# Plain products for the last pairs' spreads, second power and layer 1, a wider turn through DRAM, and a last pair finished tile by tile

## The chip, the cores and the metric

One core of a Trainium2 chip runs the whole kernel. The metric is the device time of one execution in microseconds (us), as the median of several runs. A profile is of one execution. Its span runs from the program's first to its last instruction on the core, and the execution's own time is a little longer.

## The reference

The input `x` is 64 graphs of 256 nodes and 128 features, `adj` one 256x256 matrix for all. Four graph layers follow each other, each wrapped as `x = layernorm(x + layer(x))`, all in fp32. The lines that matter here:

```python
# layer 0: a gated recurrence, five steps, with m = adj @ h
z = sigmoid(av @ w3_w.T + w3_b + u3); r = sigmoid(av @ w4_w.T + w4_b + u3)   # av = [m, m]
hv = tanh(av @ w5_w.T + w5_b + (r * h @ u5_w.T + u5_b)); h = (1 - z) * h + z * hv
# layer 1: A is a softmax over the edges' values, split in its diagonal and the rest
out = (A * I) @ (x @ W[0]) + (A * (1 - I)) @ (x @ W[1]) + bias
# layer 2: attention over adj, then a graph isomorphism layer with adj
# layer 3: a polynomial in adj of order 3, for two adjacencies that are the same one here
y = sum over k of (adj^k x) @ weight[k]
```

## The kernel before

Two graphs are a pair, and 32 pairs pass through the four layers. A pair's value is 512 columns on 128 partitions: four tiles of 128 nodes by 128 features (graph 0 first and second half, graph 1 first and second half), or their transposes.

**Order of the work.** The functions emit nothing at once. Each adds an operation with an estimated duration and the values that it reads and writes (`pe`, `act`, `dve`, `pool`, `S.add`). `Schedule.order` then lists them for all engines by a plan: of the operations that are ready it takes the one that could start first, and among these the one with the earliest due time. Due times are 15 us apart from pair to pair (10 for the last twelve) with an offset by layer (`HOLD`; layer 3 has 40 us). `SEEDS` shifts due times in windows of 15 us of planned time, a number for each window. Each engine then executes its list in order, so an instruction that waits holds back all behind it on that engine. Tiles are shared: 38 of 512 columns (A), 6 wider ones (B), 8 PSUM banks (PS), 8 DRAM buffers (E). Some operations have a choice of engines (`evacuate`: ACT or DVE; `dve_or_pool`, `sum_`: DVE or POOL).

**Spreads.** A product with a 256x256 matrix is a "spread". The plain form (`spread`, L591) has four matmuls of 256 columns. The block form (`spread7`, L609) takes seven 128-column products of sums of blocks instead of eight; the sums before are L615 to L617, those after L624, L628 and L630, and `evacuate` (L273 on ACT, L274 on DVE) copies partial results out of PSUM. `spread_on7` (products L1011, sums L1017 to L1019 and L1028 to L1032) does the same for the second power of `adj`, on top of what is already in a bank. `SEVEN` says how many of the last pairs take plain forms: `q1` layer 1's spread, `g` layer 2's, `q3` layer 3's, `a2` the second power, `pr` layer 3's weight products, which else go by `polynomial7` (products L968).

**Layer 1.** `layer1` spreads `x1`, scales `x1` by the diagonal (L808), turns that, puts `x1` and the bias into a PSUM bank (`seed`) and adds eight weight products (L764). `layer1b` multiplies the turned `x1` by both weights first (L779) and spreads after (L790). Before, `L1 = -1`, and no pair takes `layer1b`.

**Turns.** A transposition (`turn`) of most values goes through DRAM: DVE transposes 32x32 blocks (L572), one DMA stores the tile (L574), four DMAs load it back (L580), all issued by SP. The last few pairs of some sites use TensorE (L566). Site "y" is the last turn of layer 0, whose result L755 adds to `x0`; 30 pairs turn there by DMA.

**The last pair.** It goes through plain products for its two halves of the nodes (L906, L907; second power L914), and `finish` does each half: a square with its sum on ACT (L934), the variance on DVE (L937, L938), an addition (L940) and a power (L941) on POOL, the scaling on ACT (L942) and DVE (L943), and a store (L944).

Of the kernel before, what the change touches and what calls it, by code (L numbers as in the profile page):

```python
# [12 lines left out]
P = 128  # L13
# [7 lines left out]


FAST = (0, 1, 2, 3, 4)
SEVEN = {"q1": 4, "g": 4, "q3": 4, "pr": 2, "a2": 2}
FIRST, FINAL = 1, 0
L1 = -1

TURN, TT = 0.44, 0.61
LN_EPS = 1e-5
# [30 lines left out]

XLOAD, TLOAD = (0.6, 1.33, 2.5), (0.6, 1.05, 1.5)

SEEDS = [0, 113, 389, 2033, 10562, 18537, 0, 26210, 32078, 38683, 45160, 51706, 59435, 64921, 73141, 0, 83634, 0,
         0, 101285, 106383, 115324, 122347, 124837, 135500, 136596, 144091, 154692, 155685, 163406, 167552, 0,
         184910, 185838, 194559, 198013, 204219, 214550, 217961, 222675, 234550, 236036, 241268, 247877, 256254,
         259921, 269567, 275378, 0, 285335, 290367, 299853, 303332, 311190, 314874, 321452, 333089, 337426,
         340720, 349168, 0, 0, 0, 0, 0, 0, 0, 0, 0, 0, 0, 0, 426668, 0, 438032, 447771, 0, 460174, 0, 468597,
         475031, 0, 0, 497766, 503314, 0, 0, 520395, 524746, 0, 0, 545845, 549434, 555392, 562168, 571415, 574768,
         578884, 0, 0]


def mm(cols, n=1):
# [4 lines left out]
class Value:  # L77
# [3 lines left out]
    def __init__(self, cls=None, ap=None, name="v"):  # L81
        self.cls, self.ap, self.name = cls, ap, name
        self.writers, self.readers, self.left = [], [], 0


        self.seeded = self.full = False

    def at(self, *shape):

# [150 lines left out]
def kernel(ctx: ExitStack, tc: tile.TileContext, x, xT, adj, adjT, mats, cols, rows, out):  # L240
# [14 lines left out]
    def act(us, fn, r, w):  # L255
        S.add([("ACT", us, fn)], r, w)

    def dve(us, fn, r, w):
        S.add([("DVE", us, fn)], r, w)

    def dve2(us, fn, r, w):
        S.add([("DVE+", us, fn)], r, w)

    def pool(us, fn, r, w):
        S.add([("POOL-", us, fn)], r, w)
# [257 lines left out]
    def bank():  # L523

        t = Value("PS", name="ps")
        t.full = True
        return t
# [29 lines left out]
    def turn(i, name, site, n=512):  # L557


        o = Value("A", name=name) if n == 512 else i  # L560
        if not by_dma(site):
            ts = [Value("PS", name="ps") for _ in range(n // 512)]
            for k, t in enumerate(ts):
                def fn(k=k, t=t):
                    for c in range(4):
                        nc.tensor.transpose(tokens(t)[:, c, :], i.at(n // P, P)[:, 4 * k + c, :], ident.ap)  # L566
                pe(TURN, fn, [i, ident], [t])
            for k, t in enumerate(ts):
                evacuate(lambda k=k: o.at(n)[:, 512 * k:512 * k + 512], lambda t=t: t.at(512), [t], [o])
            return o  # L570
        st, d = Value("A" if n == 512 else "B", name="turn"), Value("E", name="turn")
        dve(n / 512 * 0.55 + 0.09, lambda: nc.vector.transpose(st.at(n), i.at(n)), [i], [st])  # L572
        blocks = lambda *ap: bass.AP(tensor=d.ap.tensor, offset=d.ap.offset, ap=ap)
        S.add([("SP", 0.52, lambda: nc.sync.dma_start(blocks([P, P], [P * P, n // P], [1, P]), st.at(n // P, P)))],  # L574
              [st], [d], (0.6, n / 512 * 0.86, 0.5))

        def move():
            for q in range(4):
                b = blocks([P, 32], [32 * P, n // 32], [1, 32])
                nc.sync.dma_start(o.at(n // 32, 32)[32 * q:32 * q + 32],  # L580
                                  bass.AP(tensor=b.tensor, offset=b.offset + 32 * q, ap=b.ap))
        S.add([("SP", 2.1 if n == 512 else 2.7, move)], [d], [o], (-0.8, n / 512 * 1.5, 0.9))
        return o

    def spread(i, right):
# [134 lines left out]
    def layer0(x0, hT):  # L720
        h = x0
        for s in range(STEPS):
            mT = spread7(h, aT, aT7) if s in FAST and FIRST <= S.pair < n_pairs - FINAL else to_sbuf(spread(h, aT), "mT")
            t = bank()

            def reset(t=t, hT=hT, mT=mT):
                nc.tensor.matmul(t.at(512), mat("u3"), hT.at(512), start=True, stop=False)  # L727
                nc.tensor.matmul(t.at(512), w4.ap, mT.at(512), start=False, stop=True)  # L728
            pe(mm(512, 2), reset, [Wg, w4, hT, mT], [t])
            r, z, new = (Value("A", name=n) for n in ("r", "z", "hT"))  # L730
            act(0.59, lambda t=t, r=r: nc.scalar.activation(r.at(512), t.at(512), AF.Tanh, bias=bzrh.ap[:, 1:2], scale=0.5),  # L731
                [t, bzrh], [r])
            dve2(TT, lambda r=r, hT=hT: nc.vector.scalar_tensor_tensor(r.at(512), r.at(512), 1.0, hT.at(512),
                                                                      op0=ALU.add, op1=ALU.mult), [r, hT], [r])
            pe(mm(512), lambda t=t, mT=mT: nc.tensor.matmul(t.at(512), w3.ap, mT.at(512), start=False, stop=True,  # L735
                                                            skip_group_check=True), [w3, mT, t], [t])
            act(0.59, lambda t=t, z=z: nc.scalar.activation(z.at(512), t.at(512), AF.Tanh, bias=bzrh.ap[:, 0:1], scale=0.5),  # L737
                [t, bzrh], [z])
            t = bank()

            def candidate(t=t, mT=mT, r=r):
                nc.tensor.matmul(t.at(512), w5.ap, mT.at(512), start=True, stop=False)  # L742
                nc.tensor.matmul(t.at(512), u5h.ap, r.at(512), start=False, stop=True)  # L743
            pe(mm(512, 2), candidate, [w5, u5h, mT, r], [t])

            act(0.59, lambda t=t: nc.scalar.activation(t.at(512), t.at(512), AF.Tanh, bias=bzrh.ap[:, 2:3]), [t, bzrh], [t])  # L746
            dve(TT, lambda t=t, hT=hT: nc.vector.tensor_sub(t.at(512), t.at(512), hT.at(512)), [t, hT], [t])
            dve(TT, lambda t=t, z=z: nc.vector.scalar_tensor_tensor(t.at(512), z.at(512), 1.0, t.at(512),
                                                                   op0=ALU.add, op1=ALU.mult), [t, z], [t])
            dve(TT, lambda t=t, hT=hT, new=new: nc.vector.scalar_tensor_tensor(  # L750
                new.at(512), t.at(512), 0.5, hT.at(512), op0=ALU.mult, op1=ALU.add), [t, hT], [new])
            hT = new
            h = turn(hT, "h", "h" if s < STEPS - 1 else "y")
        y = Value("A", name="y")
        dve2(TT, lambda: nc.vector.tensor_add(y.at(512), h.at(512), x0.at(512)), [h, x0], [y])  # L755
        layer_norm(y, x0)

    def products(lefts, rights, t=None):
# [132 lines left out]
    def layer3(x3, p):  # L891
        xT = turn(x3, "xT", "x3")
        qT = spread7(x3, aT, aT7) if S.pair < n_pairs - SEVEN["q3"] else to_sbuf(spread(x3, aT), "qT")
        if S.pair < n_pairs - SEVEN["pr"]:
            return polynomial7(xT, qT, p)

        rr, o = Value("A", name="rr"), Value("A", name="o")
        ts = []
        for i in range(2):
# [11 lines left out]
        for i, t in enumerate(ts):  # L911
# [2 lines left out]
                    nc.tensor.matmul(t.at(512)[:, :N], a2T.ap[:, j, i * P:(i + 1) * P], rr.at(2, N)[:, j],  # L914
                                     start=False, stop=(j == 1), skip_group_check=True)
            pe(mm(256, 2), fn, [a2T, rr, t], [t])
        if S.pair == n_pairs - 1:
            for i, t in enumerate(ts):
                finish(t, Value("A", name="last"), i, p)
            return  # L920
        s, rs = scale_stats([(t, range(i, 4, 2)) for i, t in enumerate(ts)])
        for i, t in enumerate(ts):
            scale_tokens(t, o, range(i, 4, 2), s, rs)
        store(o, p)

    def finish(t, o, i, p):

        s, st, junk = Value("S", name="ms"), Value("S", name="st"), Value("A", name="junk")
        v = lambda b: t.at(2, D)[:, b, :]
        mv = lambda b: s.at(32)[:, 2 * b:2 * b + 2]  # L930
        var, rs = (lambda: s.at(32)[:, 1:4:2]), (lambda: s.at(32)[:, 4:6])
        half = lambda b: o.at(2, D)[:, b, :]
        m0, m1, r0, r1 = Part(s), Part(s), Part(o), Part(o)
        act(0.26, lambda: nc.scalar.activation(junk.at(D), v(0), AF.Square, scale=D ** -0.5, accum_out=mv(0)[:, 1:2]), [t], [m0, junk])  # L934

        def by_dve():
            nc.vector.bn_stats(st.at(6), v(1))  # L937
            nc.vector.bn_aggr(mv(1), st.at(6))  # L938
        dve(0.27, by_dve, [t], [m1, st])
        pool(0.2, lambda: nc.gpsimd.tensor_scalar(rs(), var(), LN_EPS, None, op0=ALU.add), [m0, m1], [s])  # L940
        pool(0.7, lambda: nc.gpsimd.tensor_tensor(rs(), rs(), neg_half.ap[:, :2], op=ALU.pow), [s, neg_half], [s])  # L941
        act(0.26, lambda: nc.scalar.mul(half(0), v(0), rs()[:, 0:1]), [t, s], [r0])  # L942
        dve(0.2, lambda: nc.vector.tensor_scalar(half(1), v(1), rs()[:, 1:2], None, op0=ALU.mult), [t, s], [r1])  # L943
        S.add([("SP", 0.52, lambda: nc.sync.dma_start(out[2 * p:2 * p + 2, i * P:(i + 1) * P].rearrange("b p d -> p b d"), o.at(2, D)))],  # L944
              [r0, r1], [], (0.6, 0.5, 0.9))

    def polynomial7(xT, qT, p):

# [141 lines left out]
```

## Time and profile before

| | |
|---|---|
| median of 3 runs | 1477.62 us (1476.7 to 1477.91) |
| the profiled execution's own time | 1476.42 us |
| its span | 1474.2 us |
| PE busy | 1462.0 us, 99% |
| DVE busy | 1293.2 us, 88% |
| ACT busy | 1078.7 us, 73% |
| POOL busy | 1010.0 us, 69% |
| DMA: packets, volume, share of 16 engines | 946868, 216.70 MB, 71% |
| granted TensorE clock, mean | 0.999 |

PE is TensorE's matmuls, PEld its weight loads, DVE VectorE, ACT ScalarE, POOL GpSimd, SP the engine that issues the DMAs. "L609" is line 609 of the kernel before. A row of the timeline or of a group names the engine, the line, the operation, what it writes and reads ("ps<-aT,a"), shapes and a count; in brackets stands how long the engine was idle before it and what released it. A matmul in fp32 shows as two instructions. Ends of matmuls are modelled, and neighbours overlap in the record, so their starts tell more than their busy time.

### The profile page before, as it was taken

The numbers are of one execution on the slowest core, as the hardware profiler recorded it, in microseconds if no ns is written. First come the engines' busy times: TensorE is split into PE (matmuls) and PEld (weight loads), VectorE is DVE, ScalarE is ACT, GpSimd is POOL, SyncE is SP. The second block draws the span as 40 slices with busy tenths as digits, with TensorE's granted clock in tenths as the row PEclk, the third lists the DMA queues.
The fourth block names the chain that finished last, engine by engine and source line by source line (L and its number), as shares of the span: only waits on it lengthen the run. The fifth ranks groups of instructions, "written<-read, shape, count | busy, mean of one in ns | idle before, by whom it ended". The sixth has DMA issues, their size and how long they took to land.

```text
span 1474.2 us, 29700 instructions
## 1 busy us (share of the span) xinstructions
PE 1462.0 (99%) x8274; PEld 1068.6 (72%) x8274; DVE 1293.2 (88%) x3185; ACT 1078.7 (73%) x3315; POOL 1010.0 (69%) x1574
## 2 busy tenths in 40 slices
PE   9999999999999999999999999999999999999998
PEld 6565666667667777777668777667777677778997
DVE  7877878889999989999988988888999889899995
ACT  3444556667788788878766887666788777889896
POOL 4422445566677788877658787657778788779875
PEclk9999999999999999999999999999999999999999
DMA  7544565767788898778786677675897777766653
GB/s 227 115 103 87 119 130 117 155 133 157 152 166 168 180 187 161 164 152 165 160 157 140 143 171 159 124 152 124 170 177 158 156 146 149 160 138 135 127 106 93
DMA packets 946868, 216.70 MB, mean 147 GB/s; under 512 B 726032, under 2 KB 942224, under 8 KB 946704
## 3 DMA queue, kind: packets, MB, share of 16 engines
q1 hardware_dynamic: 946704, 214.81, 71.3%
q8 instruction: 66, 1.08, 0.3%
q14 instruction: 98, 0.80, 0.2%
HBM read 116.86 MB, written 97.85 MB: 146 GB/s over the span
## 4 chain that ended last, share of the span: by engine, by line
PE 93%; DVE 3%; POOL 2%; ACT 1%; DMA 1%; issue 1%; SPq 0%; POOLq 0%; ACTq 0%; DVEq 0%
PE ps L609 24%; PE ps L735 9%; PE ps L742 9%; PE ps L743 9%; PE ps L727 9%; PE ps L728 9%; PE ps L764 7%; PE ps L968 6%; PE ps L864 3%; PE ps L1011 3%; PE ps L591 2%; PE ps L824 2%; POOL s L696 1%; DVE b L839 0%; POOL s L651 0%
## 5 line engine op out<-in xcount | busy, mean ns | idle before, releaser
L609 PEld LDWEIGHTS ps<-aT,a 128*128 128x128 f32 x2208 | 297.3, 192 | 78.2 <-issue 69.1
L273 ACT COPY a<-ps 128x128 f32<-128x128 f32 (+2 forms) x618 | 259.5, 442 | 105.2 <-PE ps L609 49.2
L609 PE MATMUL ps<-aT,a 128*128 128x128 f32 x2208 | 324.3, 275 | 0.5 <-ACT x L708 0.5
L731 ACT ACTIVATE a<-ps,bzrh 128x512 f32<-128x512 f32 x160 | 110.5, 691 | 102.4 <-PE ps L728 92.8
L746 ACT ACTIVATE ps<-ps,bzrh 128x512 f32<-128x512 f32 x160 | 106.2, 664 | 98.0 <-PE ps L743 95.6
L628 POOL TENSOR_TENSOR a<-a 128x128 f32<-128x128 f32 x206 | 105.2, 516 | 90.8 <-DVE a L624 80.1
L742 PE MATMUL ps<-a,w 128*128 128x512 f32 x320 | 163.8, 594 | 0.0
L728 PE MATMUL ps<-a,w 128*128 128x512 f32 x320 | 163.4, 592 | 0.0
L743 PE MATMUL ps<-a,u5h 128*128 128x512 f32 x320 | 163.4, 592 | 0.0
L735 PE MATMUL ps<-a,w 128*128 128x512 f32 x320 | 162.8, 594 | 0.1
L630 DVE TENSOR_TENSOR a<-ps,a 128x256 f32<-128x256 f32 x239 | 99.1, 417 | 71.0 <-ACT a L273 42.1
L688 ACT ACTIVATE a<-ps 128x128 f32<-128x128 f32 x504 | 133.1, 289 | 29.7 <-PE ps L764 13.4
L572 DVE STREAM_TRANSPOSE a<-a 128x512 f32<-128x512 f32 x215 | 149.4, 699 | 3.7 <-POOL a L1028 0.5
L696 POOL TENSOR_TENSOR s<-s,neg_half 128x4 f32<-128x4 f32 x127 | 142.4, 1122 | 6.8
L764 PE MATMUL ps<-W,a 128*128 128x128 f32 x1024 | 142.1, 275 | 0.1
L624 POOL TENSOR_TENSOR a<-a 128x256 f32<-128x256 f32 x123 | 92.0, 750 | 72.9 <-ACT a L273 72.1
L764 PEld LDWEIGHTS ps<-W,a 128*128 128x128 f32 x1024 | 130.3, 192 | 14.5 <-issue 12.4
L737 ACT ACTIVATE a<-ps,bzrh 128x512 f32<-128x512 f32 x160 | 110.8, 692 | 37.4 <-PE ps L735 34.3
L727 PE MATMUL ps<-a,W 128*128 128x512 f32 x256 | 131.0, 593 | 0.9 <-ACT a L273 0.9
L615 POOL TENSOR_TENSOR a<-a 128x256 f32<-128x256 f32 x97 | 72.3, 746 | 64.8 <-DMA a<-e 44.2
L743 PEld LDWEIGHTS ps<-a,u5h 128*128 128x128 f32 x320 | 60.8, 190 | 76.5 <-issue 64.8
L728 PEld LDWEIGHTS ps<-a,w 128*128 128x128 f32 x320 | 60.8, 190 | 76.5 <-issue 65.3
(255 smaller groups left out, 3650.7 us busy)
## 6 DMA issues: line engine op xcount, KB each, us to landing
e<-a SPq DMA_DIRECT2D x277, 256.0 KB
a<-e SPq DMA_DIRECT2D x1108, 64.0 KB
e<-b SPq DMA_DIRECT2D x32, 512.0 KB
b<-e SPq DMA_DIRECT2D x128, 128.0 KB
x<-x_in SPq DMA_DIRECT2D x32, 256.0 KB
t<-xT_in SPq DMA_DIRECT2D x32, 256.0 KB
a<-d SPq DMA_DIRECT2D x32, 256.0 KB
y_out<-a SPq DMA_DIRECT2D x31, 256.0 KB
```

What stands on the lines that cost most here:

```text
L273: S.add([("ACT", us[0], lambda: nc.scalar.copy(o(), i())), ("DVE", us[1], lambda: nc.vector.tensor_copy(o(), i()))], r, w)
L572: dve(n / 512 * 0.55 + 0.09, lambda: nc.vector.transpose(st.at(n), i.at(n)), [i], [st])
L609: pe(mm(128), lambda: nc.tensor.matmul(blk(t, k), left(), rt(), start=start, stop=True, skip_group_check=True), [*r, right, terms, *[t] * ...
L688: nc.scalar.activation(tokens(junk)[:, c, :], v.at(len(tiles), D)[:, k, :], AF.Square, scale=D ** -0.5, accum_out=mv()[:, c, 1:2])
L696: pool(1.02, lambda: nc.gpsimd.tensor_tensor(rs(), rs(), neg_half.ap, op=ALU.pow), [s, neg_half], [s])
L727: nc.tensor.matmul(t.at(512), mat("u3"), hT.at(512), start=True, stop=False)
L728: nc.tensor.matmul(t.at(512), w4.ap, mT.at(512), start=False, stop=True)
L735: pe(mm(512), lambda t=t, mT=mT: nc.tensor.matmul(t.at(512), w3.ap, mT.at(512), start=False, stop=True, skip_group_check=True), [w3, mT, t ...
L737: act(0.59, lambda t=t, z=z: nc.scalar.activation(z.at(512), t.at(512), AF.Tanh, bias=bzrh.ap[:, 0:1], scale=0.5), [t, bzrh], [z])
L742: nc.tensor.matmul(t.at(512), w5.ap, mT.at(512), start=True, stop=False)
L743: nc.tensor.matmul(t.at(512), u5h.ap, r.at(512), start=False, stop=True)
L764: nc.tensor.matmul(tokens(t)[:, c, :], tokens(i)[:, c, :], w(), start=(first and k == c == 0), stop=(k == len(lefts) - 1), skip_group_chec ...
```

## The change

Four constants change, and three pieces of code. `a2` goes from 2 to 12: pairs 20 to 29 take the second power by plain products inside `polynomial7`. `q3` goes from 4 to 8: pairs 24 to 27 take layer 3's spread in the plain form. `L1` goes from -1 to 4: pairs 28 to 31 take `layer1b`. `SEEDS` has other numbers from its sixth place on.

`wide_turn` replaces the turn by DMA of site "y": the blocks are written by DVE in another order, so that the store has runs of 512 elements and the loads runs of 128 instead of 32. The value that comes back has its blocks permuted, and the addition after it (L755) reads it by a permuted pattern.

`by_tile` replaces the last pair's products: each of the four tiles gets a bank of its own, the right-hand factors of the second power are made and copied out first, and `finish` is called for tiles 0 and 1, then for tile 2, then for tile 3. In `finish`, a single tile has its square on ACT and its scaling on DVE; the addition moves from POOL to DVE.

```diff
-SEVEN = {"q1": 4, "g": 4, "q3": 4, "pr": 2, "a2": 2}
+SEVEN = {"q1": 4, "g": 4, "q3": 8, "pr": 2, "a2": 12}
 FIRST, FINAL = 1, 0
-L1 = -1
+L1 = 4
...
-SEEDS = [0, 113, 389, 2033, 10562, 18537, 0, 26210, 32078, 38683, 45160, 51706, 59435, 64921, 73141, 0, 83634, 0,
...
+SEEDS = [0, 113, 389, 2033, 10562, 18452, 0, 26116, 32753, 43555, 44392, 55649, 60421, 62978, 0, 78890, 82048,
...
         st, d = Value("A" if n == 512 else "B", name="turn"), Value("E", name="turn")
+        if site == "y":
+            return wide_turn(i, st, d, o)
...
+    def wide_turn(i, st, d, o):
+
+        line = lambda start, *ap: bass.AP(tensor=d.ap.tensor, offset=d.ap.offset + start, ap=ap)
+        dve(0.64, lambda: nc.vector.transpose(st.at(4, 4, 32).rearrange("p q c e -> p c q e"), i.at(4, 4, 32)), [i], [st])
+        S.add([("SP", 0.52, lambda: nc.sync.dma_start(line(0, [512, P], [1, 512]), st.at(512)))], [st], [d], (0.6, 0.63, 0.5))
+
+        def move():
+            for q in range(4):
+                nc.sync.dma_start(o.at(4, P)[32 * q:32 * q + 32], line(P * q, [512, 32], [512 * 32, 4], [1, P]))
+        S.add([("SP", 2.1, move)], [d], [o], (-0.8, 1.23, 0.9))
+        o.turned = True
+        return o
...
-        dve2(TT, lambda: nc.vector.tensor_add(y.at(512), h.at(512), x0.at(512)), [h, x0], [y])
+        halves = lambda v: v.at(4, 4, 32).rearrange("p s c e -> p c s e") if v.turned else v.at(4, 4, 32)
+        dve2(TT, lambda: nc.vector.tensor_add(halves(y), halves(h), halves(x0)), [h, x0], [y])
...
+        if S.pair == n_pairs - 1:
+            return by_tile(xT, qT, p)
...
-        if S.pair == n_pairs - 1:
-            for i, t in enumerate(ts):
-                finish(t, Value("A", name="last"), i, p)
-            return
...
+    def by_tile(xT, qT, p):
+
+        r, rr, tiles = bank(), Value("A", name="rr"), []
+
+        def product(t, o, c, k):
+            def fn():
+                nc.tensor.matmul(o(), tokens(xT)[:, c, :], vx.ap[:, k, :], start=(k == 0 or c == 0), stop=False, skip_group_check=True)
+                nc.tensor.matmul(o(), tokens(qT)[:, c, :], vq.ap[:, k, :], start=False, stop=True, skip_group_check=True)
+            pe(mm(128, 2), fn, [xT, qT, vx, vq, *[t] * (k == 1 and c > 0)], [t])
+
+        for c in range(4):
+            product(r, lambda c=c: tokens(r)[:, c, :], c, 1)
+        evacuate(lambda: rr.at(512), lambda: r.at(512), [r], [rr])
+        for c in range(4):
+            t = bank()
+            product(t, lambda t=t: t.at(D), c, 0)
+            tiles.append(t)
+        for group in ((0, 1), (2,), (3,)):
+            for c in group:
+                def fn(c=c, t=tiles[c]):
+                    for j in range(2):
+                        nc.tensor.matmul(t.at(D), a2T.ap[:, j, c % 2 * P:(c % 2 + 1) * P], tokens(rr)[:, c - c % 2 + j, :], start=False,
+                                         stop=(j == 1), skip_group_check=True)
+                pe(mm(128, 2), fn, [a2T, rr, tiles[c]], [tiles[c]])
+            finish([tiles[c] for c in group], Value("A", name="last"), group[0], p)
...
+        act(0.37, lambda: nc.scalar.activation(junk.at(D), ts[0].at(D), AF.Square, scale=D ** -0.5, accum_out=mv(0)[:, 1:2]),
+            [ts[0]], [means[0], junk])
...
+        if n > 1:
+            dve(0.5, by_dve, [ts[1]], [means[1], st])
+        dve(0.07, lambda: nc.vector.tensor_scalar(rs(), var(), LN_EPS, None, op0=ALU.add), means, [s])
+        pool(0.7, lambda: nc.gpsimd.tensor_tensor(rs(), rs(), neg_half.ap[:, :n], op=ALU.pow), [s, neg_half], [s])
+        if n > 1:
+            act(0.35, lambda: nc.scalar.mul(o.at(n, D)[:, 0], ts[0].at(D), rs()[:, 0:1]), [ts[0], s], [outs[0]])
+        dve(0.3, lambda: nc.vector.tensor_scalar(o.at(n, D)[:, n - 1], ts[n - 1].at(D), rs()[:, n - 1:n], None, op0=ALU.mult),
+            [ts[n - 1], s], [outs[n - 1]])
```

## The prediction

> **What bounds the kernel now.** I read the page's first part, then busy time by stage, then the chain of waits for the step of one matmul, then PE's timeline round its stalls, then the last ten microseconds.
>
> ```profile
> span 1474.2 us, 29700 instructions
> ...
> PE 1462.0 (99%) x8274; PEld 1068.6 (72%) x8274; DVE 1293.2 (88%) x3185; ACT 1078.7 (73%) x3315; POOL 1010.0 (69%) x1574
> ```
>
> PE is the bound, but its 1462.0 us holds waiting, because the ends of matmuls are modelled. So I measure PE by starts, from the chain (start, length, line, instructions):
>
> ```profile
> 78.76 1.72 PE ps L735 x4
> ...
> 1403.84 2.23 PE ps L1011 x20
> ...
> 1431.73 1.73 PE ps L591 x8
> ```
>
> A 512-column instruction takes 1.72/4 = 0.43 us (0.429 over longer stretches), a 128-column one 2.23/20 = 0.112, a 256-column one 1.73/8 = 0.216. A matmul in this type is two instructions. The groups of PE hold 1600, 6462 (with a few narrower) and 212 of these: 1600 x 0.429 + 6462 x 0.112 + 212 x 0.216 = 1455.9 us of pure issue. The other 18.3 us of the span: 1.2 before the first matmul; 3.2 of slow first matmuls (L333 x8 and L591 x8 take 3.78 + 2.83 in the chain, against 16 x 0.216); 5.9 after PE's last (1468.3); some 8 of stalls. The stalls lie in two places:
>
> ```profile
> 1300.00:1350.00 50.00, 50.00 (x363) 42.67 (x361) 47.81 (x129) 45.19 (x162) 42.30 (x61) 1.00 0.62 127
> 1350.00:1400.00 50.00, 47.48 (x384) 45.49 (x383) 48.35 (x147) 45.72 (x176) 45.47 (x64) 1.00 0.65 137
> 1400.00:1450.00 50.00, 49.90 (x408) 48.43 (x407) 46.31 (x147) 43.54 (x175) 37.20 (x60) 1.00 0.53 108
> ```
>
> Columns: stretch, its length, busy PE, PEld, DVE, ACT, POOL. From 1300 on DVE is busy for 96%, ACT and POOL for about 90%: the last pairs' layers 1 to 3 load the vector engines as much as PE. There PE waits:
>
> ```profile
> 1349.74 0.39 PE L609 MATMUL ps<-ginT,a 128*128 128x128 f32 x2
> 1351.38 1.99 PE L591 MATMUL ps<-offT,x 128*128 128x256 f32 x8 [1.25 <-DVE a L750]
> ...
> 1389.91 0.61 PE L824 MATMUL ps<-wpx,a 128*128 128x130 f32 x4
> 1391.02 0.71 PE L968 MATMUL ps<-vq,a 128*128 128x128 f32 x4 [0.50 <-DVE a L985]
> ```
>
> Start to start, less the steps, 1.42 us is lost at 1350 (two steps of 0.112 should have ended at 1349.96) and 0.66 at 1390; 0.71 more at 1368, before another L591 that ACT's L273 releases. L750, L273 and L985 read PSUM, so PE waits for results or banks that a late vector engine holds. Five more of 0.2 to 0.3 and many small ones bring 1345 to 1420 to 4.9 us. The other place is 485 to 534: four stalls, 0.53, 1.06, 0.54 and 0.66, sum 2.8, released by a DMA, ACT, POOL and ACT. The tail:
>
> ```profile
> 1468.30 0.28 ACT L934 ACTIVATE a<-ps 128x128 f32<-128x128 f32 x1 [0.35 <-PE ps L914]
> ...
> 1468.70 0.30 DVE L937 BATCH_NORM_STATS2 s<-ps 128x6 f32<-128x128 f32 x1 [0.20 <-ACT a L934]
> ...
> 1469.98 0.71 POOL L941 TENSOR_TENSOR s<-s,neg_half 128x2 f32<-128x2 f32 x1
> ...
> 1471.13 0.35 DVE L943 TENSOR_SCALAR a<-ps,s 128x128 f32<-128x128 f32 x1 [0.66 <-ACT a L942]
> ```
>
> From PE's last result (1468.3) to the last scaled tile (1471.48) are 3.2 us, because ACT and DVE take turns on one bank, then POOL's addition and power, then ACT, then DVE. The store takes the rest.
>
> **What the Trainium skill says.** Perfetto Trace Analysis, Identifying the Most-Contended Engine, says that matmul busy time is no measure of headroom because matmuls are pipelined; the 6 us between 1462.0 and 1455.9 agree. TensorE: Matmul & The Clock Gate, Back-to-back issue gap, gives an isolated gap of N/2.4 + 2.5 ns: 56, 109 and 216 ns for 128, 256 and 512 columns. This trace shows twice that for each instruction, so what carries over is that cost goes with columns. PSUM — Partial Sum Buffer, PSUM bank collisions raise a hardware error, says that no two engines may be in one bank at the same time; the DVE wait on L934 above, for a square of the other half of the same bank, agrees. DMA: Bandwidth & Descriptors, Specifications, puts line rate at 512 B and more; here 726032 of 946868 packets are below 512 B.
>
> **The change, part by part.** All prices below are PE steps or rows of this trace.
>
> Second power (a2 2 to 12): pairs 20 to 29 drop spread_on7. Seven block products are 14 x 0.112 = 1.57 us of PE; the plain form is 8 x 0.216 = 1.73. Each costs +0.16, ten +1.6. What goes from the vector engines, at DVE's durations: 0.42 (L1017), 0.28, 0.28 (L1018, L1019), 0.58 (the copy of L273), 0.42, 0.42 (L1028, L1029), 0.28 (L1031) and 0.69 (L1032): 3.4 us a pair, 34 in all, more where POOL has it (0.73 and 0.46 for the sums).
>
> Layer 3's spread (q3 4 to 8): pairs 24 to 27, again +0.16 each, +0.7. Vector work: L615 0.42, L616 and L617 0.28 each, copies 0.58 and 0.29, L624 0.42, L628 0.28, L630 0.42, less one copy of 0.58: 2.4 a pair, 10 in all.
>
> Layer 1 of the last four pairs: PE had 8 x 0.216 for the spread and 16 x 0.112 for the products, 3.52; layer1b has 16 x 0.216 = 3.46: -0.06 each, -0.2. The copy of 0.58, the scaling L808 of 0.69 and the seed of about 0.6 give way to two copies of 0.37 and two additions of about 0.42: -0.3 a pair, about -1. The transposition by DMA, with its store and four loads on SP, stays, now of x1 itself, and all products wait for it; before, the spread could start at once. Queued behind it on PE is the planned next product; the many layer-3 products of that stage cover it. Bound without cover: one turn for the last pair, DVE's 0.70 and the issues of 0.38 and 1.92 with their landings, some 5 us.
>
> The last pair, by_tile: 32 x 0.112 instead of 16 x 0.216 for the products, 16 x 0.112 instead of 8 x 0.216 for the power: +0.1 and +0.1. One copy of R lies under the second set of products (1.8 us), so the 0.2 us that L914 waits for ACT goes. Tail: the last tile's square and its read of the sum take 0.5, DVE's addition about 0.1, the power, by the rows for 2 and 4 columns (0.71, 1.04), about 0.55 for one column; the three powers queue on POOL, so the last ends near +1.7; DVE's scaling 0.35 ends it near +2.1 against +3.2. I take -1.1; bounds -1.6 (half the bytes in the last store) and 0 (POOL or SP late for three small groups).
>
> The turn of "y" (30 pairs): same bytes, same five issues on SP, but the reads become 512 B and the writes 2 KB: 30 x 1920 = 57600 packets fewer, 6%. Hidden: of PE's named waits one, 0.4 us, is a DMA's. The permuted patterns of the DVE transpose (0.70) and the addition L755 (0.68) aren't in this trace; I price them as the plain ones, bounds 0 and +0.35 an instruction (half of its own time), on DVE where it has 12% idle and other pairs' work covers it. In time: 0, from -0.5 to +0.5.
>
> The seeds: from the sixth window of 15 us on, the order is another one. No row prices that. The stalls it makes may be anything from none to twice the present.
>
> Sum against the profiled run's own 1476.4 us (span 1474.2 and 2.2 around it): PE work +1.6 +0.7 -0.2 +0.2 = **+2.3**; L914 -0.2; tail -1.1; stalls after 1345: 45 us of work leave three engines that are over 90% busy, so I keep 1.4 of 4.9, **-3.5**; stalls before: -0.5 for lighter DMA, a guess between -2.8 and +5. Sum -3.0: 1473.4. The median of the runs stands 1.2 above the profiled one (1477.6), so **1474.6**.
>
> **Rivals.** (A) The vector backlog goes, as summed: 1474.6; at best no stall is left, 2.3 - 1.3 - 7.9 = -6.9, 1470.7. For it: the three largest late stalls are all released by vector work. (B) PE's added work stays and the stalls do too, since in-order queues make new ones elsewhere: 2.3 - 1.3 = +1.0, 1478.6. For it: DVE is as busy from 400 to 600 (186 of 200 us) and few stalls come of it, so load alone doesn't explain them. (C) Slower: the new order puts PE behind late inputs more often, as between 485 and 534 where every stall has another releaser, or before the last pairs' turned x1. A stall there costs 0.5 to 1.1; six more at 0.7 are +4.2, with B's +1.0 some +5, 1482.8. It decides as soon as stalls add 2 us to the present 8. Against it: less vector work and fewer packets make inputs earlier.
>
> **How the numbers follow.** About 0.2% (3 us) is what a measurement of this kernel can tell from no change. (A) has about 0.6, and its centre lies on that bound, so it splits: 0.44 faster, 0.16 within. (B) has 0.22, of which 0.01 faster, 0.2 within and 0.01 slower. (C) has 0.18, all slower. Together 0.45, 0.36, 0.19. The likeliest is (A), 1474.6, its own range 1470.7 to 1477. The range for 8 in 10 reaches from 1470.5 through (B) into (C), to 1481.0.
>
> **What would show it.** PE instructions fall by 14 x 6 for the block products and 4 x 8 for layer 1 and rise by 24 in by_tile, net 92 fewer, while pure issue rises by 2.3. Right if DVE from 1300 to 1450 falls from 142.5 by more than 10 us and PE's starts there have under 2 us of stalls; if the last DVE scaling ends about 2.1 us after PE's last result; if small packets fall by some 60000. Wrong if stalls of 4 us or more remain after 1345, or new ones stand elsewhere, or PE waits for the last pairs' turns.

## The result, and the profile after

| | before | changed |
|---|---|---|
| median of 6 runs | 1476.74 us (1475.14 to 1477.91) | 1470.93 us (1469.22 to 1473.5) |
| ratio | | 0.9964, 95% interval 0.9954 to 0.9975 |
| the profiled execution's own time, its span | 1476.42, 1474.2 us | 1470.14, 1468.4 us |

The changed kernel is 0.36% faster by the ratio (0.25 to 0.46%, so 3.7 to 6.8 us) and 5.8 us faster by the medians; 3.0 were forecast. The head of its page:

```profile
span 1468.4 us, 29324 instructions
...
PE 1460.4 (99%) x8182; PEld 1066.6 (73%) x8182; DVE 1266.6 (86%) x3140; ACT 1061.7 (72%) x3271; POOL 997.3 (68%) x1544
...
DMA packets 889283, 216.69 MB, mean 148 GB/s; under 512 B 664608, under 2 KB 880800, under 8 KB 889120
```

PE has 92 instructions fewer, DVE is busy 26.6 us less, and there are 57585 packets fewer for the same bytes. Still, nothing here tells where 5.8 us went: PE is at 99% in both kernels. The busy time by stage does (stretch, length, then busy PE, PEld, DVE, ACT and POOL):

```profile
1300.00:1350.00 50.00, 50.00 (x348) 42.33 (x348) 46.46 (x133) 43.83 (x166) 42.16 (x66) 1.00 0.71 142
1350.00:1400.00 50.00, 50.00 (x360) 47.46 (x359) 47.09 (x150) 46.84 (x181) 37.46 (x51) 1.00 0.73 150
1400.00:1450.00 50.00, 50.00 (x359) 47.38 (x358) 34.86 (x111) 39.80 (x165) 22.71 (x35) 1.00 0.49 101
```

PE no longer waits in this stage, while DVE and POOL have room in its last third. Up to 1400, where the three largest late stalls of before stood (1350, 1368 and 1390), DVE is nearly as full as it was: 46.46 and 47.09 us against 47.81 and 48.35. ACT has 46.84 from 1350 on, more than before's 45.72, and only POOL clearly less, 37.46 against 45.47. So the busy shares alone don't say that a lighter load took those three away. The tail, by the timeline:

```profile
1461.69 1.95 PE L961 MATMUL ps<-a,a2T 128*128 128x128 f32 x16
...
1463.23 0.30 DVE L976 BATCH_NORM_STATS2 s<-ps 128x6 f32<-128x128 f32 x1 [0.34 <-PE ps L961]
...
1463.87 1.22 POOL L981 TENSOR_TENSOR s<-s,neg_half 128x1 f32<-128x1 f32 x2 [0.34 <-DVE s L980]
...
1465.12 0.35 DVE L984 TENSOR_SCALAR a<-ps,s 128x128 f32<-128x128 f32 x1 [0.32 <-POOL s L981]
```

By these rows PE's last result is there at 1463.64 (1461.69 + 1.95) and the last tile is scaled at 1465.47: 1.8 us instead of 3.2. The plan put the two single tiles first and the pair of tiles last, and ACT, DVE and POOL work beside each other, as each tile has its own bank.

To set the runs side by side I take all PE instructions of a trace in order of start and subtract from each distance to the next start the step of its shape (0.112, 0.216 or 0.429 us, by 128, 256 or 512 columns). What remains is stall, or steps that run slower than that: in the column to 1450 such slow steps make up 1.7 us in e8, 1.6 in e3, 3.3 in e4 and 4 to 5 in e1 (the last section shows how they look). Small negative sums are rounding. "Pure issue" is a count of instructions times their steps, up to the start of PE's last instruction. The labels e1 to e13 are the runs of the next section. Us, from one profiled execution each:

| kernel | pure issue | stalls to 50 | 50 to 1300 | 1300 to 1450 | later | from PE's last start on | span |
|---|---|---|---|---|---|---|---|
| before | 1455.7 | 3.2 | 2.6 | 4.9 | 0.3 | 6.3 | 1474.2 |
| changed | 1458.0 | 3.6 | 0.7 | -0.1 | 0.0 | 5.0 | 1468.4 |
| before, lighter vector work (e7) | 1455.7 | 3.3 | 0.1 | 2.6 | 0.3 | 6.3 | 1469.5 |
| changed, dummy load (e8) | 1458.0 | 3.3 | -0.5 | 16.8 | 1.5 | 5.0 | 1485.3 |
| dummy load on DVE alone (e10) | 1458.0 | 3.0 | 1.3 | 7.0 | 0.3 | 5.0 | 1475.7 |
| on POOL alone (e11) | 1458.0 | 2.3 | 2.0 | 6.0 | 0.0 | 5.0 | 1474.5 |
| on ACT alone (e12) | 1458.0 | 3.5 | 2.5 | -0.1 | 0.0 | 5.0 | 1470.1 |
| before with wide turn (e5) | 1455.7 | 3.5 | 1.0 | 4.6 | 0.3 | 6.3 | 1472.7 |
| changed with old turn (e13) | 1458.0 | 4.0 | 4.5 | -0.3 | 0.0 | 5.0 | 1472.4 |
| before with by_tile (e6) | 1456.0 | 3.9 | 1.3 | 14.9 | 0.1 | 4.8 | 1482.2 |
| before, three constants (e1) | 1457.7 | 2.9 | 3.9 | 15.2 | 0.3 | 6.3 | 1487.5 |
| blocks kept, seeds chosen anew (e9) | 1456.0 | 3.6 | -0.3 | 9.3 | 0.0 | 6.2 | 1476.0 |
| before, seeds zero (e3) | 1455.7 | 4.3 | 7.8 | 12.9 | 2.4 | 6.2 | 1490.5 |
| changed, seeds zero (e4) | 1458.0 | 4.5 | 7.6 | 11.8 | -0.1 | 4.8 | 1487.8 |

The columns add up to the span with the 1.2 us before PE's first matmul. From before to changed: +2.3 of PE work, -5.0 of stalls from 1300 to 1450, -0.3 later and -1.3 in the tail, -1.9 of stalls from 50 to 1300, +0.4 at the start. (PE's last instruction has 256 columns before and 128 after; with its own step counted as work, these are +2.2 and -1.2.) The middle is uncertain, for executions differ in it: e7 and e5 have PE's order of before and show 0.1 and 1.0 where before shows 2.6, and e12 has the changed kernel's and shows 2.5 against 0.7. Of the four stalls between 485 and 534 that the forecast names, those at 486 and 494 are missing from e5, e6 and e7 too, although e6 and e7 keep the old turn and, so far, the old order. So the traces support the late stalls and the tail as places of the gain, but no sure gain in the middle.

### The profile page after: what moved, and what is told of

The parts are those of the page before. It is cut to its first block, busy times and chain, and to the rows that moved or that the text cites. A ratio compares the mean times of both kernels' runs of the same rounds, so it can differ in the third digit from the quotient of the medians.

```text
span 1468.4 us, 29324 instructions
## 1 busy us (share of the span) xinstructions
PE 1460.4 (99%) x8182; PEld 1066.6 (73%) x8182; DVE 1266.6 (86%) x3140; ACT 1061.7 (72%) x3271; POOL 997.3 (68%) x1544
## 4 chain that ended last, share of the span: by engine, by line
PE 95%; POOL 2%; DVE 1%; DMA 1%; ACT 1%; issue 0%; SPq 0%; POOLq 0%; DVEq 0%
PE ps L624 24%; PE ps L757 9%; PE ps L742 9%; PE ps L743 9%; PE ps L758 9%; PE ps L750 9%; PE ps L780 7%; PE ps L1010 6%; PE ps L880 4%; PE ps L1053 2%; PE ps L840 2%; PE ps L606 2%; PE ps L1036 1%; POOL a L630 0%; PE ps L806 0%; PE ps L795 0%
## 5 line engine op out<-in xcount | busy, mean ns | idle before, releaser
L624 PEld LDWEIGHTS ps<-aT,a 128*128 128x128 f32 x2176 | 292.9, 192 | 80.8 <-issue 70.5
L273 ACT COPY a<-ps 128x512 f32<-128x512 f32 (+2 forms) x605 | 252.6, 437 | 116.3 <-PE ps L624 55.8
L624 PE MATMUL ps<-aT,a 128*128 128x128 f32 x2176 | 318.6, 275 | 0.8 <-DVE a L630 0.6
L639 POOL TENSOR_TENSOR a<-a 128x256 f32<-128x256 f32 x131 | 96.2, 737 | 76.2 <-ACT a L273 68.8
L780 PE MATMUL ps<-W,a 128*128 128x128 f32 x960 | 135.4, 275 | 0.0
L780 PEld LDWEIGHTS ps<-W,a 128*128 128x128 f32 x960 | 123.8, 192 | 13.8 <-issue 11.7
L643 POOL TENSOR_TENSOR a<-a 128x128 f32<-128x128 f32 x194 | 95.9, 498 | 52.7 <-DVE a L639 47.4
L574 DVE STREAM_TRANSPOSE a<-a 128x512 f32<-128x512 f32 x181 | 125.2, 695 | 2.4 <-PE ps L624 0.4
L631 POOL TENSOR_TENSOR a<-a,a 128x128 f32<-128x128 f32 x134 | 70.3, 525 | 63.9 <-DVE a L630 54.3
```

The lines of the kernel that those rows point to most:

```text
L273: S.add([("ACT", us[0], lambda: nc.scalar.copy(o(), i())), ("DVE", us[1], lambda: nc.vector.tensor_copy(o(), i()))], r, w)
L624: pe(mm(128), lambda: nc.tensor.matmul(blk(t, k), left(), rt(), start=start, stop=True, skip_group_check=True), [*r, right, terms, *[t] * ...
L780: nc.tensor.matmul(tokens(t)[:, c, :], tokens(i)[:, c, :], w(), start=(first and k == c == 0), stop=(k == len(lefts) - 1), skip_group_chec ...
```

## The experiments

The question was whether the late stalls went because vector work went, as the forecast said, or because the seeds gave another order. Ratios are to the kernel before on the same chip (1474.4 to 1474.7 us there). A difference to the changed kernel is the difference of the ratios, since it ran on another chip, and is uncertain by about 2 us.

**Lighter vector work in the old order (e7).** In `spread_on7` for pairs 20 to 29, and in layer 3's `spread7` for pairs 24 to 27:

```diff
-            spread_on7(rr, y)
+            spread_on7(rr, y, 4 if S.pair >= n_pairs - 12 else P)
...
-        dve(TT, lambda: nc.vector.tensor_add(y.at(512), y.at(512), m.at(512)), [y, m], [y])
+        dve(TT, lambda: nc.vector.tensor_add(y.at(4, P)[:, :, :w], y.at(4, P)[:, :, :w], m.at(4, P)[:, :, :w]), [y, m], [y])
```

> The kernel before with its order kept on every engine. For the pairs whose block products the change drops, the sums, copies and additions round these products are cut to 4 of 128 columns (all of the second power's for pairs 20 to 29; of layer 3's spread for pairs 24 to 27 all but one copy), so this part is not computed; the matmuls stay. Theory (vector backlog): PE's stalls after 1345 us, 4.9 us, fall to under 1.5, and the run is 3 to 5 us faster than before. Rival (the order makes the stalls, not the load): the stalls stay within 1 us of 4.9 and the time within 1 us.

Measured 1472.94 us, ratio 0.9990 (0.9983 to 0.9996), 1.5 us faster. The late stalls fell from 4.9 to 2.6, between both expectations. Of the three largest, those at 1368 and 1390 (0.70 and 0.66 us) are gone. The first stays, 1.25 us instead of 1.42, before the same line and with the same releaser:

```profile
1346.75 0.83 PE L609 MATMUL ps<-ginT,a 128*128 128x128 f32 x6
1348.67 1.99 PE L591 MATMUL ps<-offT,x 128*128 128x256 f32 x8 [1.08 <-DVE a L750]
```

One stage line shows how far DVE and POOL were relieved later:

```profile
1400.00:1450.00 50.00, 50.00 (x404) 48.65 (x404) 36.56 (x138) 40.76 (x177) 29.16 (x57) 1.00 0.47 99
```

DVE has 36.56 here and the changed kernel 34.86; POOL 29.16 and 22.71. From 1300 to 1350 there is little relief, 47.20 for DVE against 47.81. So lighter vector work with the order kept takes away about half of the late stalls. The sums stay in place in this run, only shorter, so PE still waits for each chain of them, which the plain forms do without; that share isn't measured.

The stall that stays stands before layer 1's spread of one of the last four pairs. In the changed kernel these pairs go by `layer1b`, and no PE row of that form (`offT`, x, 256 columns) is left in its trace. No run has `layer1b` alone with an order kept or fitted, so whether it or the seeds took this stall away is not shown.

**The load put back into the new order (e8, e10, e11, e12).** The changed kernel keeps its order; at each plain product of the same pairs it issues dummy sums and copies (here for a second power; a layer-3 spread gets fewer):

```diff
+        for n in dve_:
+            nc.vector.tensor_add(extra[0].ap[:, :n], two[:, :n], two[:, :n])
+        for n in pool_:
+            nc.gpsimd.tensor_add(extra[1].ap[:, :n], two[:, :n], two[:, :n])
+        for n in act_:
+            nc.scalar.copy(extra[2].ap[:, :n], two[:, :n])
...
+                    if i == 0:
+                        more((256, 256, 256, 256), (256, 128, 128, 128), (128, 128))
                     for j in range(2):
```

> The changed kernel with its order kept, and beside it, for the same pairs, dummy sums and copies of about the dropped sizes on DVE, POOL and ACT (into scratch, nobody waits for them). Theory (vector backlog): stalls come back after 1250 us, 2 to 5 us in sum, and the run is that much slower than the changed kernel (about 1473 to 1476). Rival (order): under 1 us slower.

Measured 1487.74 us, ratio 1.0087 (1.0073 to 1.0101), 1.2% above the changed kernel: some 18 us, far more than the 2 to 5 expected. In this trace one stall after another stands from 1367 on, mostly released by DVE. The dummies are not the dropped work in size: by the pages of the next three runs they add 21 us to DVE, 29 to POOL and 6 to ACT, where the change takes 27, 13 and 17 away. And each product's come in one burst. Then one engine at a time; each of the three kernels keeps one of the loops of `more` and drops the other two. DVE:

```diff
-        for n in pool_:
-            nc.gpsimd.tensor_add(extra[1].ap[:, :n], two[:, :n], two[:, :n])
-        for n in act_:
-            nc.scalar.copy(extra[2].ap[:, :n], two[:, :n])
```

> The changed kernel, order kept, with the dummy load for the same pairs on DVE alone (four sums of 256 columns for a second power, two for a layer-3 spread: about 20 us in all). Theory (DVE is the fullest engine of the last stage and its late results hold PE): most of the loss of the full load, 8 to 14 us slower than the changed kernel. Rival (POOL's long instructions make the loss): under 4 us.

Measured 1478.33 us, ratio 1.0024 (1.0015 to 1.0034): 0.6% or 9 us above the changed kernel, as expected for the theory.

> The changed kernel, order kept, with the dummy load on POOL alone (one sum of 256 and three of 128 columns a pair and product, about 2.1 us each time, 29 us in all). Theory: POOL has room in that stage, 2 to 5 us slower than the changed kernel. Rival (POOL decides): 8 us or more.

Measured 1476.6 us, ratio 1.0015 (1.0008 to 1.0023): 0.5% or 7.5 us. The expected 2 to 5 was too little, and the rival's 8 is within the uncertainty, although POOL was busy for only 37.46 of 50 us without this load. The stage line with it, where PE loses 3 us:

```profile
1350.00:1400.00 50.00, 47.05 (x340) 44.06 (x338) 46.35 (x135) 44.00 (x171) 44.20 (x67) 1.00 0.69 141
```

The largest of its stalls, 1.92 us, shows how idle time on POOL can be no help:

```profile
1365.42 2.04 POOL L559 TENSOR_TENSOR extra<-aT 128x256 f32<-128x256 f32 x4
...
1367.42 1.04 POOL L675 TENSOR_TENSOR s<-s,neg_half 128x4 f32<-128x4 f32 x1
...
1368.49 1.22 DVE L677 SCALAR_TENSOR_TENSOR s<-s 128x4 f32<-128x4 f32 x1 [1.93 <-POOL s L675]
...
1369.71 0.41 DVE L851 TENSOR_TENSOR h<-ps,hbias 128x260 f32<-128x260 f32 x1
...
1370.17 1.13 PE L615 MATMUL ps<-aT,x 128*128 128x256 f32 x4 [1.76 <-DVE h L851]
```

The burst of dummies (L559) holds up the power of a normalization (L675), DVE stands still until that is done, and what PE needs (L851) stands behind it in DVE's list. For such a stall it counts when POOL delivers, not how busy it is.

> The changed kernel, order kept, with the dummy load on ACT alone (copies of about 0.6 us for a second power, 0.3 for a spread, 7 us in all). Both: 0 to 2 us slower than the changed kernel. If it is more, ACT is as tight as DVE.

Measured 1470.45 us, ratio 0.9972 (0.9963 to 0.9981): 0.1% or 1 us, and no late stall. By the medians the three add up to what e8 shows, 18 us; by the table's stalls after 1300 they make 13 of its 18. So with the order fixed, added work on DVE or POOL brings stalls of 6 to 7 us back, and 6 us on ACT bring none. This is how sensitive the new order is, not what the dropped work is worth: sizes and places differ, and the order was fitted to a kernel without the dummies. How much of the loss is this misfit isn't shown.

**The order alone, and an order not fitted (e6, e1, e3, e4, e9).** First the tile-by-tile last pair alone in the kernel before (`by_tile` and the new `finish`, nothing else).

```diff
+        if S.pair == n_pairs - 1:
+            return by_tile(xT, qT, p)
...
-        if S.pair == n_pairs - 1:
-            for i, t in enumerate(ts):
-                finish(t, Value("A", name="last"), i, p)
-            return
```

> The kernel before with the tile-by-tile last pair alone; the order is the same but for the last part. Theory: from PE's last matmul to the end 1.1 to 1.3 us less, the stall of 0.2 us in the last power gone, PE's work 0.2 more: 1.1 to 1.3 us faster in all. Rival (the small groups queue on POOL and SP): no faster.

Measured 1483.99 us, ratio 1.0063 (1.0049 to 1.0077): 9.6 us slower, where 1.1 to 1.3 us faster was expected. Its tail is 1.5 us shorter, about as expected, but the longer list of operations of the last pair moves others in the last seventh of PE's order, and late stalls rise from 4.9 to 14.9:

```profile
1350.00:1400.00 50.00, 44.20 (x342) 41.02 (x341) 48.72 (x149) 42.72 (x165) 41.53 (x61) 1.00 0.62 127
1400.00:1450.00 50.00, 45.03 (x368) 43.33 (x368) 44.43 (x126) 41.61 (x171) 39.78 (x56) 1.00 0.50 101
```

The load is about that of before, and the order differs: the same seeds now shift other operations, and the order that comes out is a worse one. The three constants alone, which change PE's order from 774 us on, point the same way:

```diff
-SEVEN = {"q1": 4, "g": 4, "q3": 4, "pr": 2, "a2": 2}
+SEVEN = {"q1": 4, "g": 4, "q3": 8, "pr": 2, "a2": 12}
-L1 = -1
+L1 = 4
```

> The kernel before with the three constants alone (plain second power, layer 3's spread and layer 1 for the same last pairs), seeds, turn and finish as before. Theory (an order that is not fitted again costs more than the lighter work gains, as with the tile-by-tile finish alone): 5 us or more slower than before, with stalls after 1250 us. Rival (lighter vector work gains whatever the order): 1 to 4 us faster than before.

Measured 1488.37 us, ratio 1.0091 (1.0077 to 1.0106): 14 us slower, as the theory said, with 15.2 us of late stalls and slow steps in spite of the lighter work. With all seeds zero neither kernel has a fitted order:

```diff
-SEEDS = [0, 113, 389, 2033, 10562, 18537, 0, 26210, 32078, 38683, 45160, 51706, 59435, 64921, 73141, 0, 83634, 0,
...
+SEEDS = [0]
```

> The kernel before with all seeds zero: plain due times, an order fitted to nothing. Both theories: slower than before, by 10 us or more, the loss as stalls of PE, mostly after 1250 us. To be set against the next run.

Measured 1493.13 us, ratio 1.0123 (1.0108 to 1.0139).

> The changed kernel with all seeds zero. Theory (less vector work needs less fitting): 4 us or more faster than the kernel before with zero seeds, by fewer stalls after 1250 us, although PE's work is 2.3 us more. Rival (the gain is in the seeds): within 2 us of it, or slower.

Measured 1489.81 us, ratio 1.0107 (1.0093 to 1.0121): 3.3 us faster than e3, a little under the 4 expected, and with overlapping intervals. By the profiles 1.4 us of that is the tail and 3.6 are stalls after 1300, less 2.3 of PE work. Only 1.1 of the 3.6 lie before 1450. Then an order fitted again with the block products kept: wide turn (planned costs as before), `by_tile`, and new `SEEDS` from the 81st window on, chosen by the shortest planned end. So e9 is e6 with two edits more:

```diff
+        if site == "y":
+            return wide_turn(i, st, d, o)
...
-SEEDS = [0, 113, 389, 2033, 10562, 18537, 0, 26210, 32078, 38683, 45160, 51706, 59435, 64921, 73141, 0, 83634, 0,
...
+SEEDS = [0, 113, 389, 2033, 10562, 18537, 0, 26210, 32078, 38683, 45160, 51706, 59435, 64921, 73141, 0, 83634, 0,
...
```

> The kernel before with the wide turn and the tile-by-tile last pair, the block products kept, and the seeds of the last twenty windows chosen anew for it by the shortest planned end, so that the order fits. Theory (fitting the order isn't enough, the dropped vector work is what clears the stalls): stalls after 1345 us of 3 to 6 us stay, the tail is 1.5 us shorter, in all 0 to 3 us faster than before. Rival (the order alone clears them): stalls under 1.5 us, 4 us or more faster than before, and so as fast as the changed kernel, which has 2.1 us more of PE work.

Measured 1477.84 us, ratio 1.0025 (1.0016 to 1.0034): 3.5 us slower than before, and neither expectation holds. Late stalls went from 14.9 to 9.3, not to the 4.9 of before; the tail was no shorter than before's, as pair 30's power and scalings stood in front of the last pair's. This order, chosen by its planned end, runs worse than before's own fitted one, so e9 doesn't test the best that an order can do with the old work: the rival that an order alone clears the stalls is neither borne out nor excluded.

**The wide turn (e5, e13).** First in the kernel before, with the old planned costs, so that every engine keeps its order:

```diff
+        if site == "y":
+            return wide_turn(i, st, d, o)
```

> The kernel before with the wide turn of y alone, its planned costs left as they were so that the order on every engine is the one of before. Theory: DMA time is hidden; within 1 us of before, the four stalls from 485 to 534 us stay at about 2.8 us, the DVE transpose and addition take 0.70 and 0.68 us as before, some 58000 packets fewer. Rival (lighter DMA removes those stalls): 2 to 3 us faster. Other rival (permuted patterns are slower): transpose and addition at 1 us, no change in the time.

Measured 1473.49 us, ratio 0.9992 (0.9984 to 1.0000): 0 to 2 us faster, no clear gain. Of the four stalls that were to stay, two are gone, but they are gone from e7 with the old turn as well. Then the reverse in the changed kernel, again with its order kept: the wide turn's planned costs, the old accesses.

```diff
-        S.add([("SP", 0.52, lambda: nc.sync.dma_start(line(0, [512, P], [1, 512]), st.at(512)))], [st], [d], (0.6, 0.63, 0.5))
+        S.add([("SP", 0.52, lambda: nc.sync.dma_start(blocks([P, P], [P * P, 4], [1, P]), st.at(4, P)))], [st], [d], (0.6, 0.63, 0.5))
```

> The changed kernel, order kept on every engine, with the old turn of y (runs of 128 elements in the store, 32 in the loads) in place of the wide one. Theory (DMA time is hidden): within 1.5 us of the changed kernel, no stall of over 1 us back before 1300 us. Rival (the order leans on the faster turn): 3 us or more slower, with PE waiting for a DMA or for the addition after the turn.

Measured 1471.44 us, ratio 0.9978 (0.9971 to 0.9984): 0.14% or 2 us slower than the changed kernel, with an uncertainty nearly as large, so between both expectations. Against the theory, two stalls of over 1 us stand before 1300. One of 1.63 at 621 is in e12 too, with the wide turn. In the other PE waits for a DMA, as it does for 0.35 us at 473:

```profile
520.87 0.39 PE L781 MATMUL ps<-W,a 128*128 128x128 f32 x2
522.17 1.80 PE L781 MATMUL ps<-W,a 128*128 128x128 f32 x14 [0.92 <-DMA a<-e]
```

L781 doesn't read what the turn of "y" brings back, which goes to an addition on DVE, so this is the DMA of another turn. Whether the heavier transfers of "y" held it up isn't shown.

The permuted patterns cost nothing on DVE. In the changed kernel (minimum, median, maximum in ns; 0.70 and 0.68 us were the plain ones):

```profile
L590 DVE STREAM_TRANSPOSE a<-a x30: 667/701/712, 142.7 to 1292.3; 128x512 f32<-128x512 f32 x30
...
L771 DVE TENSOR_TENSOR a<-a,x x32: 644/682/1751, 152.2 to 1351.7; 128x512 f32<-128x512 f32 x32
```

## Why the prediction was right or wrong, point by point

The measured 1470.93 us lies in the stated range, but near its lower end (1470.5) and close to rival (A)'s best case of no stall at all (1470.7); the forecast was the middle, 1474.6.

**PE's added work: right.** Forecast +2.3 us and 92 instructions fewer; counted +2.2 to +2.3 and 92. (Unrounded, the forecast's own terms make 2.2: four times 0.16 is 0.6, not 0.7.) The count times the steps of before is no measurement of its own; that the steps hold is shown by the stretch from 1300 to 1450, where nothing is left over.

**The tail: right.** Forecast -1.1 with the last scaling 2.1 us after PE's last result; measured 1.8 us and -1.2 to -1.3 to the end. e6 shows the same part alone, -1.5. The 0.2 us of L914's wait went as forecast.

**The late stalls: right cause in part, wrong size.** This term of the sum was -3.5, with 1.4 us kept; it measured -5.0, and nothing stayed. These 1.5 us and 1.4 of the middle are what the forecast lacked. Its reason, that the vector engines' backlog is lifted, has support where the order is fixed: e7 takes 2.3 us of stalls away, and e10 and e11 bring 6 to 7 back. But the reason was incomplete. Of DVE's relief from 1300 to 1450, 14.1 us, 11.5 stand after 1400, behind the largest stalls, and the premise of three engines over 90% busy was a misreading for POOL, whose lines give 85, 91 and 74%. The largest stall, at 1350, outlasts the lighter load in e7; the order or `layer1b` took it. And the forecast treated the order as an uncertainty around the load. e6 and e1 show that with orders that don't fit, the late column is 15 us with either load. The changed kernel has its gain with a lighter load, other forms and an order fitted to them, together. How much each would be worth alone can't be given: lighter work in the old order gave 1.5 us, and with the old work the best order on record is before's own, with 4.9 us of late stalls. That the fit left no late stall at all was luck as far as the forecast goes, for it had no price for the order.

**The middle: a guess, and still unsettled.** The term was -0.5. The traces show -1.9, less than executions of one order differ among themselves (before 2.6, e7 0.1). The lighter DMA may help by 0 to 2 us (e5; e13 says the same with more uncertainty), so that "hidden" is neither shown nor refuted.

**The rivals.** (B), added work without relief, is out: the late stalls are gone. (C), a slower order, didn't come, but was the right thing to fear: e6, e1, e3 and e4 are what it described, late inputs before an in-order PE, at two to four times its price of some 5 us. One of its two places was the last pairs' wait for the turned x1. In the changed kernel no stall stands there (before L795). With orders that don't fit, stalls do stand before that product: 1.3 and 3.1 us in e1, and 0.6, 2.0 and 2.9 in e4. The profile puts them down to DVE and ACT and not to a DMA, so that the turn itself made them isn't shown.

## What to carry to other kernels

Where one engine is near its limit and others are almost as full, look for its stalls start to start, stage by stage, since its busy share hides them; work that is a little dearer on the bound engine can pay if it empties the ones that feed it, as here together with a new order. When the order comes from a plan with fitted numbers, an edit and its refit are one change: an edit that shortens the tail by 1.5 us, tried with the old numbers, was 10 us slower here. To find which engine's load matters, put dummy work on one at a time with the order kept; choose its size and places like those of the work in question, or it shows only how tight that engine's deliveries are.

## What the runs showed of the hardware that was not expected

A stall can be followed by a cost beyond its length. In e8, after stalls of 1.35 and 1.40 us within five microseconds, PE ran at half its rate for a while; the next rows are its timeline.

```profile
1430.11 1.62 PE L793 MATMUL ps<-W,a 128*128 128x128 f32 x8 [1.24 <-ACT ps L273]
1431.52 3.15 PE L619 MATMUL ps<-ginT,a 128*128 128x256 f32 x8
1434.50 0.61 PE L1023 MATMUL ps<-vt,a 128*128 128x128 f32 x4
```

The eight instructions of L619 take 2.98 us from start to start instead of 8 x 0.216 = 1.73, and the stage view gives a granted clock of 0.66 from 1430 to 1435. e1 shows the same after a stall of 3.1 us, e4 after two of 2.0 and 2.9, and e3 after one of 2.3. The clock records of these traces give half the clock for 3.41 us at a time in e8, e3 and twice in e4, and for three times as long, 10.24 us, in e1. The length of the stall alone doesn't decide it: after 2.2 us in e10 (at 1406) and 2.4 in e1 (at 1403) the clock stayed at 1.00. What does is open. In the changed kernel such steps stand at the start alone.

POOL was the other surprise: with about a quarter of its time idle, 29 us more work on it cost 7.5 us; in the largest of the stalls a short result that DVE needed stood 2 us behind it.
